# Node-ordered score columns, and a single transfer for the row maxima, in a four-layer graph network

## The chip, the cores and the metric

The kernel runs on one core of a Trainium2 chip. The metric is the device time of one execution in microseconds; lower is better. The engines are TensorE (PE; its weight loads are shown apart as PEld), VectorE (DVE), ScalarE (ACT), GpSimd (POOL) and SyncE (SP), which only issues transfers. Each runs its own instructions in order and waits for the others through semaphores. All arithmetic is in float32.

## The reference

There are B = 32 samples with N = 512 nodes and F = 64 features, and one adjacency `adj` (512 x 512, mostly zeros, with ones on the diagonal before scaling). Four residual layers follow each other: a plain graph convolution, a two-step one, a graph attention layer, and layer 3, which the change touches:

```python
def gat_layer(x, graph, W, b):
    h = x @ W
    s = jnp.einsum('bnd,bmd->bnm', h, h) * graph
    s = jnp.where(s == 0.0, NEG_INF, s)
    a = jax.nn.softmax(s, axis=2)
    return jnp.einsum('bnm,bmd->bnd', a, h) + b

h = jnp.maximum(_layernorm(x, axis=-1), 0.0)
heads = jax.vmap(lambda W, b: gat_layer(h, adj, W, b))(Wh, bh)   # 8 heads of width 128
cat = jnp.moveaxis(heads, 0, 2).reshape(B, N, H * D)
o = jax.nn.leaky_relu(cat, negative_slope=0.01)
out = gat_layer(o, adj, W_out, b_out)                           # one more, width 64
x = x + jax.nn.leaky_relu(out, negative_slope=0.01)
```

The scores of a head are symmetric before the softmax: `h h^T` with `h = x W` is `x M x^T` with `M = W W^T`, which the kernel keeps as `m2`. So a row's maximum is also the maximum of the column of the same node.

## The kernel before

Layers 0 to 2 take the first 460 us and are in a stage of their own (`slot`, `drain`). In them the change touches only `masks`, which writes `flow_neg`, a mask of -1e16 where `adj` is zero.

Nodes are laid over the 128 partitions so that node `4 p + c` sits on partition `p` in block `c` (C = 4 blocks). A row of 512 columns in **block order** holds the four nodes of a block's partitions one after the other: column `c * 128 + p`. In the **nodes' own order** it would be column `4 p + c`. Before the change every row of layer 3 is in block order.

Layer 3 is cut into 144 units, objects of a class `Pair`: 128 `Heads` (a sample and two heads at a time) and 16 `Out` (the output layer of two samples). They stand in a list `flow`, eight `Out` among the `Heads` (units 15 to 78, nine apart) and the other eight at the end. `planned` gives the order of work: the function `period(t)` is called for every t and issues, for units at different ages, what the five engines do, in an order written out by hand that is kept on every engine. `unit(k)` is the unit that is k periods old; negative ages are units that are still to come. For one unit:

- ages -4 to -1: `features`, `make_hx` (L521) make the sample's features `hx` in block order; `make_g` (L528) multiplies them by `m2`, and ScalarE copies the product from PSUM to `g` (L549). For an `Out`, `make_gs` (L621) scales the kept product `gT` by `urow` on GpSimd into `gs`.
- ages -1 and 0: `scores(r)` (L368) for the four row blocks r: TensorE multiplies a 128-column block of `terms()[0]` as weights with all 512 columns of `terms()[1]`, for two heads (k) at once. `maxima(r)` (L378) on VectorE adds the mask, turns the sign and keeps the row maximum in a column of `top`. The scores' PSUM pool `ps_s` has two buffers, which the scores share with the odd exponentials (`e_ps`).
- age 0: `spread_out` (L390): VectorE turns `top` (128 partitions x 8 used columns) in blocks of 32 x 32, and SP sends four transfers of 8 rows x 128 bytes to `top_row` in DRAM. `totals_out(0, sync)` of the unit of age 2 follows on SP (`parts`, L448), and then `spread_in` (L399), which waits for `top_row` and reads it back to all partitions as `topb`, 512 KB.
- age 1: four times `shift` (L407) on GpSimd, which subtracts `topb` from the scores column by column (the scores are used as columns, with the maximum of the column's node); `exps` on ScalarE (L416); `join` on VectorE (L419), which adds an odd block to the even block before it and frees the PSUM that the odd exponentials took. `make_v` of an `Out` (L610) transposes `gT` into the values `gV`, `gD`.
- age 2: `totals` (L432) and `values` (L421) on TensorE, `parts` to all partitions, the reciprocals, `rec_row` to DRAM (L461).
- age 3: `recb` back (L468), and `normalize` on VectorE (L474), which makes `o_att`.
- age 4: a `Heads` makes `y` and `cat` (L551 to L576), of which `product` (L596) accumulates the output layer's input, kept by `keep_product` (L606) in `gT`. An `Out` adds its bias (`bias`, L640), transposes back (`back`, L643), and at ages 5 and 6 adds to `x` on GpSimd and stores.

Three pools matter: `ps_m` (two PSUM buffers, tag "m") is shared by `g_ps`, `hx_ps`, `tot_ps`, `y_ps`, `gV_ps` and `back_ps`; `pairs_b` (L1266) holds `cat` and `y`, one buffer of 128 x 1024 in each period; `wk` holds `gs`, `topb`, `recb`, `o_att`.

Of the kernel before, what the change touches and what calls it, by code (L numbers as in the profile page):

```python
# [8 lines left out]
F32 = mybir.dt.float32  # L9
AF = mybir.ActivationFunctionType  # L10
OP = mybir.AluOpType
# [3 lines left out]
P = 128  # L15
LN_EPS = 1e-5
GAT_NEG = -9000000000000000.0
FLOW_NEG = -1e16
# [4 lines left out]
def fast_form(  # L23
# [25 lines left out]
    nc = tc.nc  # L49
    B, N, F = x.shape  # L50
    C = N // P
    H, _, D = w_heads.shape
# [3 lines left out]
    Q = P // 32  # L56

    const = ctx.enter_context(tc.tile_pool(name="const", bufs=1))
    xpool = ctx.enter_context(tc.tile_pool(name="xpool", bufs=1))
    tiny = ctx.enter_context(tc.tile_pool(name="tiny", bufs=4))  # L60
# [14 lines left out]
    adj_p = setup.tile([P, C, C, P], F32, name="adj_p")  # L75
# [37 lines left out]
    b_out2 = const.tile([P, 1], F32, name="b_out2")  # L113
# [27 lines left out]
    adj_f = adj_p.rearrange("p c k q -> p c (k q)")  # L141
    flow_neg = const.tile([P, C, N], F32, name="flow_neg")
# [15 lines left out]
    E_MAX = 5.0  # L158

    def masks():  # L160
        nc.vector.tensor_scalar(flow_neg, adj_f, 0.0, FLOW_NEG, op0=OP.is_equal, op1=OP.mult)

    root_d = const.tile([P, C], F32, name="root_d")
    urow = const.tile([P, N], F32, name="urow")
# [29 lines left out]
    def judge_rows(c):  # L194
        both, t = row_pair("edge"), row_pair("t")[:, 0]
        ok, edge = both[:, 1], both[:, 0]
        nc.vector.tensor_scalar(edge, adj_f[:, c], 0.0, None, op0=OP.not_equal)
        nc.vector.scalar_tensor_tensor(
            t, urow, root_d[:, c : c + 1], edge, op0=OP.mult, op1=OP.mult
        )  # L200
        nc.vector.tensor_tensor(t, t, adj_f[:, c], OP.subtract)
        nc.vector.scalar_tensor_tensor(t, t, -1.0, t, op0=OP.mult, op1=OP.max)
        nc.vector.scalar_tensor_tensor(
            ok, adj_f[:, c], 4e-7, t, op0=OP.mult, op1=OP.is_ge
        )
        nc.vector.scalar_tensor_tensor(
            edge, adj_t[:, c], 0.0, edge, op0=OP.not_equal, op1=OP.is_equal
        )
        nc.vector.tensor_reduce(
            sound[:, 2 + C + c : 3 + C + c], both.rearrange("p k n -> p (k n)"), AX.X, OP.min  # L210
        )

    def halves(k):
        return slice(k * F, (k + 1) * F)

    def row_pair(name):

        return pairs_of[0].tile([P, 2, N], F32, name=name, tag="row")


    acc_of, pairs_of = [], []

    def acc(name, shape):
        return acc_of[0].tile(shape, F32, name=name, tag=acc_of[1])
# [82 lines left out]
    LATE = 7  # L307
    ROOM = 6

    tops = [const.tile([P, 32], F32, name=f"top{i}") for i in range(2)]  # L310
    for t in tops:
        nc.gpsimd.memset(t, 0.0)
    ones = const.tile([P, 32], F32, name="ones32")
    nc.gpsimd.memset(ones, 1.0)

    class Pair:
# [15 lines left out]
        def make_g(self):  # L332
            pass

        def make_gs(self):
            pass

        def judge_product(self):
            pass
# [7 lines left out]
        def bias(self):  # L347
            pass
# [19 lines left out]
        def scores(self, r):  # L368
            g, x = self.terms()
            ps = ps_s.tile([P, 2, N], F32, name="s_ps", tag="s")  # L370
            self.s_ps[r] = ps
            for k in range(2):
                nc.tensor.matmul(  # L373
                    ps[:, k], lhsT=g[halves(k), r * P : (r + 1) * P], rhs=x[halves(k), :],
                    start=True, stop=True,
                )

# [10 lines left out]
                )  # L388

        def spread_out(self):  # L390
            t = tiny.tile([P, 32], F32, name="top_t")
            nc.vector.transpose(t, self.top)
            self.top_row = dram.tile([2 * C, P], F32, name="top_row")
            for q in range(Q):
                nc.sync.dma_start(
                    self.top_row[:, q * 32 : (q + 1) * 32], t[q * 32 : q * 32 + 2 * C, :]
                )

        def spread_in(self):  # L399
            self.topb = wk.tile([P, 2, N], F32, name="topb")  # L400
            nc.sync.dma_start(
                self.topb.rearrange("p k n -> p (k n)"),
                self.top_row.rearrange("(o r) p -> o (r p)", o=1).to_broadcast([P, 2 * N]),
            )

        def shift(self, r, engine):
# [69 lines left out]
    class Heads(Pair):  # L476
# [51 lines left out]
        def make_g(self):  # L528
            if self.b % 2:
                return  # L530
            pss = [acc("g_ps", [P, N]) for k in range(2)]
            for k in range(2):
                u = self.pair[k]
                u.x = Heads.hx[u.b]
                u.hnv = Heads.hn[u.b]
                u.hdv = Heads.hd[u.b]
                nc.tensor.matmul(  # L537
                    pss[k],
                    lhsT=m2[halves(k), 2 * u.i : 2 * u.i + 2, :].rearrange(
                        "p h f -> p (h f)"  # L540
                    ),
                    rhs=u.x[halves(k), :],
                    start=True,
                    stop=True,
                )
            for k in range(2):
                u = self.pair[k]
                u.g = early.tile([P, N], F32, name="g", bufs=3)
                nc.scalar.copy(u.g, pss[k])  # L549

        def y_pe(self):  # L551
            self.y = []
# [25 lines left out]
        def terms(self):  # L578
            return self.g, self.x
# [7 lines left out]
    class Out(Pair):  # L587
# [17 lines left out]

        def keep_product(self):  # L606
            self.gT = wk.tile([P, N], F32, name="gT", bufs=LATE + 1)
            nc.scalar.copy(self.gT, self.gps)

        def make_v(self):  # L610
            ps = ps_m.tile([P, C, P], F32, name="gV_ps", tag="m")
# [9 lines left out]
        def make_gs(self):  # L621
            self.gs = wk.tile([P, N], F32, name="gs")
            nc.gpsimd.tensor_tensor(self.gs, self.gT, urow, OP.mult)

        def judge_product(self):
            nc.vector.tensor_reduce(
# [2 lines left out]
            )  # L629

        def terms(self):
            return self.gs, self.gs

        def v(self, k, j):
            return self.gV[:, j, halves(k)]
# [2 lines left out]
            return self.gD[:, j // 2, halves(k)]  # L638

        def bias(self):  # L640
            nc.scalar.activation(self.o, self.o, AF.Identity, bias=b_out2, scale=1.0)

        def back(self):  # L643
            self.ps = ps_m.tile([P, C, 2, F], F32, name="back_ps", tag="m")
# [145 lines left out]
    for b in range(0, B, 2):  # L790
        out_unit = Out(b)
        for i in range(H // 2):
            pair = [Heads(b + k, i) for k in range(2)]
            for k in range(2):
                u = pair[k]
# [22 lines left out]
    with (  # L818
# [94 lines left out]
        def project(terms, tag):  # L913
            p = ps_o.tile([P, C, 2, F], F32, name=tag, tag="po")
            for c in range(C):
                for i, (t, w) in enumerate(terms):
                    nc.tensor.matmul(  # L917
                        p[:, c],
                        lhsT=t[:, c * P : (c + 1) * P],
                        rhs=w,  # L920
                        start=(i == 0),
                        stop=(i == len(terms) - 1),
                    )
            return p
# [316 lines left out]
        with tc.manual_schedule(  # L1241
            engines={
                mybir.EngineType.PE,
                mybir.EngineType.DVE,
                mybir.EngineType.Activation,
            }
        ):
            start()
            begun = {
                0: gat_weights,  # L1250
                1: edges,
                2: masks,
                3: flow_weights,
                4: scales,
            }
            for c in range(C):
                begun[6 + 2 * c] = lambda c=c: judge_rows(c)
            begun[7 + 2 * C] = judge
            for k in range(M + 1):
                slot(k, begun.get(k))  # L1260
            drain()
# [1 line left out]
    setup_ctx.close()  # L1263


    pairs_of[:] = [ctx.enter_context(tc.tile_pool(name="pairs_b", bufs=H - 2))]  # L1266
    pbuf = ctx.enter_context(tc.tile_pool(name="pbuf", bufs=4 * C - 2))

    wk = ctx.enter_context(tc.tile_pool(name="work_b", bufs=2))
    dram = ctx.enter_context(  # L1270
        tc.tile_pool(name="dram", bufs=4, space=bass.MemoryType.DRAM)
    )
# [537 lines left out]
def gnn_stack_kernel(tc: tile.TileContext, *args: bass.AP):  # L1810
    nc = tc.nc
    with tc.tile_pool(name="flag", bufs=1) as pool:
        again = pool.tile([1, 1], mybir.dt.int32, name="again")
        fast_form(tc, *args, again)
        with tc.If(nc.values_load(again[0:1, 0:1])):
            general_form(tc, *args)
# [35 lines left out]
```

## Time and profile before

| | us |
|---|---|
| median of 3 runs | 2057.39 (2053.95 to 2059.52) |
| profiled execution | 2057.15 |
| its span | 2055.4 |
| layer 3's shifts on GpSimd (L407), busy | 1338.4, in 572 instructions of 2.37 |
| layer 3's maxima on VectorE (L385), busy | 726.8, in 1152 of 0.69 |
| layer 3's scores on TensorE (L373), busy | 518.8 in 2048 records |
| transfers `top_row` | 576 of 1 KB |
| transfers `topb` | 144 of 512 KB |

"Busy" is the time in which at least one instruction of the group runs. An instruction's place in the time is read from the timeline, what it waited for from the waits; a wait for several semaphores is put down to the one that came last. Matmul ends are modelled, so the idle time of TensorE is a lower bound. A float32 matmul stands in the records as two.

### The profile page before, as it was taken

How to read it: one execution, taken by the hardware profiler on the slowest of the kernel's cores; microseconds unless marked ns; L12 is line 12 of the kernel's file. 1: busy time of each engine (PE TensorE's matmuls, PEld its weight loads, DVE VectorE, ACT ScalarE, POOL GpSimd, SP SyncE). 2: the span in 40 equal slices, each digit the busy share in tenths (PEclk: the TensorE clock that was granted, in tenths of full speed). 3: DMA queues.
4: the chain of work that ended last, by engine and by line, in shares of the span. 5: the costliest groups of instructions: out<-in, count | busy, mean ns of one | idle time of the engine just before them, and what ended most of it. 6: DMA issues, size and time to landing. Idle time of an engine off the chain costs nothing.

```text
span 2055.4 us, 32929 instructions
## 1 busy us (share of the span) xinstructions
PE 1977.7 (96%) x11038; PEld 805.5 (39%) x11038; DVE 1777.2 (86%) x4261; ACT 1221.0 (59%) x1944; POOL 1422.7 (69%) x693
## 2 busy tenths in 40 slices
PE   6999999997999999999999999999999999999995
PEld 4577766662333333333333333333333333333231
DVE  5799997768999899899989998989898898889994
ACT  3443443335666666667666667666676666665554
POOL 2000000006898989899988989898888888889996
PEclk9999999989999999999999999999999999999999
DMA  5000000002222222222222222222222222222223
GB/s 142 1 1 2 1 1 1 1 1 69 74 69 79 79 78 75 79 80 78 74 84 76 82 69 84 76 73 79 76 77 69 79 74 69 79 74 79 69 84 80
DMA packets 135780, 129.33 MB, mean 63 GB/s; under 512 B 92793, under 2 KB 98081, under 8 KB 135473
## 3 DMA queue, kind: packets, MB, share of 16 engines
q1 hardware_dynamic: 116368, 126.35, 19.5%
q10 hardware_dynamic: 18720, 0.59, 0.5%
q8 instruction: 88, 1.44, 0.3%
q0 software_dynamic: 512, 0.20, 0.1%
q14 instruction: 92, 0.75, 0.1%
HBM read 119.48 MB, written 5.37 MB: 61 GB/s over the span
## 4 chain that ended last, share of the span: by engine, by line
PE 68%; POOL 9%; DVE 9%; DMA 6%; issue 3%; ACT 3%; SPq 1%; POOLq 0%; ACTq 0%; DVEq 0%
PE s_ps L373 17%; PE av L425 16%; POOL p_att L407 9%; PE nt_ps L897 8%; PE acc L990 6%; PE tot_ps L437 4%; DVE p_att L385 4%; PE gT_ps L600 4%; PE y_ps L555 4%; PE g_ps L537 3%; DMA topb<-top_row 2%; DVE p_att L419 2%; ACT e_ps L416 1%; PE po L917 1%; DMA recb<-rec_row 1%
## 5 line engine op out<-in xcount | busy, mean ns | idle before, releaser
L407 POOL TENSOR_TENSOR p_att<-p_att,topb 128x1024 f32<-128x1024 f32 x572 | 1338.4, 2374 | 201.6 <-DMA topb<-top_row 144.2
L385 DVE CUSTOM_DVE_ANT_0 p_att<-s_ps,flow_neg 128x512 f32<-128x512 f32 x1152 | 726.8, 686 | 67.2 <-PE s_ps L373 66.2
L373 PE MATMUL s_ps<-hx,g 64*128 64x512 f32 x2048 | 518.8, 615 | 27.3 <-DVE p_att L419 25.0
L416 ACT ACTIVATE p_att<-p_att 128x1024 f32<-128x1024 f32 x288 | 304.3, 1057 | 219.7 <-POOL p_att L407 209.3
L419 DVE TENSOR_TENSOR p_att<-e_ps,p_att 128x1024 f32<-128x1024 f32 x288 | 342.4, 1200 | 66.7 <-ACT e_ps L416 65.3
L416 ACT ACTIVATE e_ps<-p_att 128x1024 f32<-128x1024 f32 x288 | 295.4, 1028 | 141.1 <-POOL p_att L407 123.3
L373 PEld LDWEIGHTS s_ps<-hx,g 64*128 64x128 f32 x2048 | 175.4, 186 | 342.2 <-DVE top L385 168.8
L425 PE MATMUL av<-p_att,hd 128*64 128x512 f32 x1024 | 269.6, 605 | 0.3 <-DVE o_att L474 0.2
L425 PE MATMUL av<-p_att,hn 128*64 128x512 f32 x1024 | 263.1, 592 | 0.0
L1066 POOL TENSOR_TENSOR x<-x,bias_b 128x512 f32<-128x512 f32 x16 | 20.3, 1276 | 282.5 <-DVE hn L839 282.5
L573 DVE SCALAR_TENSOR_TENSOR cat<-y_ps,bh,cat 128x512 f32<-128x512 f32 x256 | 179.9, 744 | 0.0
L565 ACT ACTIVATE cat<-y_ps,bh 128x512 f32<-128x512 f32 x256 | 161.7, 682 | 30.1 <-PE y_ps L555 28.4
L437 PE MATMUL tot_ps<-p_att,ones 128*32 128x512 f32 x1152 | 155.5, 604 | 4.4 <-DVE p_att L419 4.4
L555 PE MATMUL y_ps<-o_att,wh_sb 64*128 64x512 f32 x512 | 132.3, 590 | 0.0
L600 PE MATMUL gT_ps<-cat,wo_sb 128*64 128x512 f32 x512 | 131.6, 592 | 0.0
L425 PEld LDWEIGHTS av<-p_att,hn 128*64 128x64 f32 x1024 | 73.5, 137 | 146.2 <-issue 146.2
L425 PEld LDWEIGHTS av<-p_att,hd 128*64 128x64 f32 x1024 | 62.1, 136 | 165.8 <-issue 133.3
L990 PE MATMUL acc<-v,s 64*128 64x65 f32 x2048 | 123.9, 279 | 0.7 <-DVE s L976 0.4
L990 PEld LDWEIGHTS acc<-v,s 64*128 64x128 f32 x2048 | 120.9, 194 | 5.9 <-DVE o L1006 1.2
L897 PE MATMUL nt_ps<-adj_t,hn 128*128 128x512 f32 x256 | 117.0, 600 | 0.8 <-DVE hn L861 0.8
L474 DVE TENSOR_TENSOR o_att<-av,recb 128x512 f32<-128x512 f32 x144 | 94.8, 659 | 16.8 <-DMA recb<-rec_row 16.3
L549 ACT COPY g<-g_ps 128x512 f32<-128x512 f32 x128 | 69.4, 588 | 66.9 <-PE g_ps L537 66.9
(182 smaller groups left out, 1984.9 us busy)
## 6 DMA issues: line engine op xcount, KB each, us to landing
topb<-top_row SPq DMA_DIRECT2D x144, 512.0 KB
recb<-rec_row SPq DMA_DIRECT2D x288, 128.0 KB
top_row<-top_t SPq DMA_DIRECT2D x576, 1.0 KB
out_dram<-y SPq DMA_DIRECT2D x32, 128.0 KB
x<-in_x_dram SPq DMA_DIRECT2D x3, 1024.0 KB
parts<-tot ACTq DMA_DIRECT2D x144, 4.0 KB
parts<-tot SPq DMA_DIRECT2D x144, 4.0 KB
rec_row<-rec_flow SPq DMA_DIRECT2D x144, 4.0 KB
```

The costliest lines, as they stand in the source:

```text
L373: nc.tensor.matmul(ps[:, k], lhsT=g[halves(k), r * P : (r + 1) * P], rhs=x[halves(k), :], start=True, stop=True,)
L385: nc.vector.tensor_tensor_reduce(out=self.p[r][:, k], in0=ps[:, k], in1=flow_neg[:, r], scale=-1.0, scalar=BIG, op0=OP.add, op1=OP.min, ac ...
L407: engine.tensor_tensor(self.p[r], self.p[r], self.topb, OP.subtract)
L416: nc.scalar.activation(to, self.p[r], AF.Exp, scale=-1.0)
L419: nc.vector.tensor_tensor(self.p[r], self.joined, self.p[r - 1], OP.add)
L425: nc.tensor.matmul(self.av[halves(k), :], lhsT=self.v(k, j) if j % 2 else self.less_next(k, j), rhs=self.p[j][:, k], start=(j == 0), stop= ...
L437: nc.tensor.matmul(ps[q : q + 32, :], lhsT=ones, rhs=self.p[2 * e + 1][:, k], start=True, stop=True,)
L555: nc.tensor.matmul(ps, lhsT=wh_sb[halves(k), 2 * self.i + k, :], rhs=self.o[halves(k), :], start=True, stop=True,)
L573: nc.vector.scalar_tensor_tensor(self.cat[:, k], self.y[k], bh[:, h : h + 1], self.cat[:, k], op0=OP.add, op1=OP.max,)
L600: nc.tensor.matmul(self.gps[halves(k), :], lhsT=wo_sb[:, h, :], rhs=Heads.cat.pop((self.b + k, h)), start=(h == 0), stop=(h == H - 1),)
L897: nc.tensor.matmul(p, lhsT=lhs(k), rhs=adj_t[:, k, :], start=(k == 0), stop=(k == C - 1))
L990: nc.tensor.matmul(self.acc[k][:, r], lhsT=self.s[b // 2][halves(k), b % 2, r * P : (r + 1) * P], rhs=self.v[halves(k), b], start=(b == 0) ...
```

## The change

In layer 3 the columns of the scores, and all that is made from them, stand in the nodes' own order; the rows stay in block order. With that, the maxima of partition p, blocks 0 to 3, are four neighbouring words of `top_row`, and one transfer takes `top` from its partitions to DRAM in pieces of 16 bytes. For that

- `g` is written in the nodes' order by ScalarE (out of PSUM in block order), and the scores take `hx` as weights and `g` as the moving operand, where it was the other way round;
- `flow_neg` is written in the nodes' order, one block at a time;
- the transpose of `top` on VectorE and three of the four transfers go; `top` shrinks from 32 to 8 columns, and isn't cleared at the start;
- for an `Out`, the kept product is turned back to block order as it is copied (`gT`), `gs` is copied once more by ScalarE into `gn` in the nodes' order, and the bias writes a new tile in block order;
- `pairs_b` has five buffers for six.

```diff
     def masks():
-        nc.vector.tensor_scalar(flow_neg, adj_f, 0.0, FLOW_NEG, op0=OP.is_equal, op1=OP.mult)
+        for c in range(C):
+            nc.vector.tensor_scalar(
+                by_blocks(flow_neg[:, c]), adj_p[:, c], 0.0, FLOW_NEG,
+                op0=OP.is_equal, op1=OP.mult,
+            )
...
+    def by_blocks(row):
+        return row.rearrange("p (i c) -> p c i", c=C)
+
+    def in_blocks(row):
+        return row.rearrange("p (c i) -> p c i", c=C)
...
-    tops = [const.tile([P, 32], F32, name=f"top{i}") for i in range(2)]
-    for t in tops:
-        nc.gpsimd.memset(t, 0.0)
+    tops = [const.tile([P, 2 * C], F32, name=f"top{i}") for i in range(2)]
...
                 nc.tensor.matmul(
-                    ps[:, k], lhsT=g[halves(k), r * P : (r + 1) * P], rhs=x[halves(k), :],
+                    ps[:, k], lhsT=x[halves(k), r * P : (r + 1) * P], rhs=g[halves(k), :],
                     start=True, stop=True,
                 )
...
         def spread_out(self):
-            t = tiny.tile([P, 32], F32, name="top_t")
-            nc.vector.transpose(t, self.top)
-            self.top_row = dram.tile([2 * C, P], F32, name="top_row")
-            for q in range(Q):
-                nc.sync.dma_start(
-                    self.top_row[:, q * 32 : (q + 1) * 32], t[q * 32 : q * 32 + 2 * C, :]
-                )
+            self.top_row = dram.tile([2, N], F32, name="top_row")
+            nc.sync.dma_start(
+                self.top_row.rearrange("k (p c) -> p k c", c=C),
+                self.top.rearrange("p (k c) -> p k c", k=2),
+            )
...
-                nc.scalar.copy(u.g, pss[k])
+                nc.scalar.copy(by_blocks(u.g), in_blocks(pss[k]))
...
         def keep_product(self):
             self.gT = wk.tile([P, N], F32, name="gT", bufs=LATE + 1)
-            nc.scalar.copy(self.gT, self.gps)
+            nc.scalar.copy(
+                self.gT.rearrange("p (c i) -> p i c", c=C),
+                self.gps.rearrange("p (i c) -> p i c", c=C),
+            )
...
             nc.gpsimd.tensor_tensor(self.gs, self.gT, urow, OP.mult)
+            self.gn = wk.tile([P, N], F32, name="gn")
+            nc.scalar.copy(by_blocks(self.gn), in_blocks(self.gs))
...
         def terms(self):
-            return self.gs, self.gs
+            return self.gn, self.gs
...
         def bias(self):
-            nc.scalar.activation(self.o, self.o, AF.Identity, bias=b_out2, scale=1.0)
+            o = wk.tile([P, N], F32, name="o_att")
+            nc.scalar.activation(
+                o.rearrange("p (c i) -> p i c", c=C),
+                self.o.rearrange("p (i c) -> p i c", c=C),
+                AF.Identity, bias=b_out2, scale=1.0,
+            )
+            self.o = o
...
-    pairs_of[:] = [ctx.enter_context(tc.tile_pool(name="pairs_b", bufs=H - 2))]
+    pairs_of[:] = [ctx.enter_context(tc.tile_pool(name="pairs_b", bufs=H - 3))]
```

More of the change, by code (lines that the diff above doesn't have):

```diff
@@ L402, in spread_in @@
                 self.topb.rearrange("p k n -> p (k n)"),
-                self.top_row.rearrange("(o r) p -> o (r p)", o=1).to_broadcast([P, 2 * N]),
+                self.top_row.rearrange("(o k) n -> o (k n)", o=1).to_broadcast([P, 2 * N]),
             )
```

## The prediction

> **What bounds the kernel now.** I read the page's busy table first, then the windows view of the stage that the change touches, then the waits of single engines in it, and last the timeline of two units of work. "Period" is the time of one of the 144 units of layer 3.
>
> ```profile
> PE 1977.7 (96%) x11038; PEld 805.5 (39%) x11038; DVE 1777.2 (86%) x4261; ACT 1221.0 (59%) x1944; POOL 1422.7 (69%) x693
> 540.00:1940.00 1400.00, 1384.77 (x6540) 450.97 (x6536) 1261.01 (x3137) 933.41 (x1436) 1241.13 (x571) 1.00 0.25 76
> PE s_ps L373 <- DVE p_att L419: 14.4, 19, 1.2
> POOL p_att L407 <- DMA topb<-top_row: 132.5, 96, 3.8
> ```
>
> In the middle of layer 3 (540 to 1940 us, the second line: PE, PEld, DVE, ACT, POOL) TensorE is idle for only 1400 - 1384.8 = 15.2 us. Nearly all of that is one wait: the score matmuls waiting for the join L419 to free their PSUM (14.4 us, 19 times). GpSimd waits much more, 132.5 us for the maxima (`topb`), but it isn't the bound. The timeline confirms it (start, duration, engine):
>
> ```profile
> 1208.98 0.21 DVE L392 STREAM_TRANSPOSE top_t<-top 128x32 f32<-128x32 f32 x1
> 1209.22 1.35 SPq L395 DMA_DIRECT2D top_row<-top_t  x4
> 1210.62 0.57 SPq L448 DMA_DIRECT2D parts<-tot  x1
> 1211.53 0.34 SPq L401 DMA_DIRECT2D topb<-top_row  x1
> 1213.23 0.14 PEld L425 LDWEIGHTS av<-p_att,hn 128*64 128x64 f32 x2 [0.28 <-issue]
> 1213.66 0.14 PEld L425 LDWEIGHTS av<-p_att,hn 128*64 128x64 f32 x2 [0.29 <-issue]
> 1214.09 0.14 PEld L600 LDWEIGHTS gT_ps<-cat,wo_sb 128*64 128x64 f32 x2 [0.29 <-issue]
> 1214.52 0.14 PEld L600 LDWEIGHTS gT_ps<-cat,wo_sb 128*64 128x64 f32 x2 [0.29 <-issue]
> 1215.45 9.36 POOL L407 TENSOR_TENSOR p_att<-p_att,topb 128x1024 f32<-128x1024 f32 x4 [1.22 <-DMA topb<-top_row]
> 1216.64 1.07 ACT L549 COPY g<-g_ps 128x512 f32<-128x512 f32 x2 [1.35 <-PE g_ps L537]
> 1218.25 0.16 PEld L437 LDWEIGHTS tot_ps<-p_att,ones 128*32 128x32 f32 x8 [0.76 <-ACT g L549]
> 1225.64 0.34 SPq L461 DMA_DIRECT2D rec_row<-rec_flow  x1
> 1227.07 1.11 SPq L468 DMA_DIRECT2D recb<-rec_row  x2
> ```
>
> TensorE's weight loads follow each other every 0.43 us without a gap, so a period of about 10.8 us is TensorE's own work. GpSimd's four shifts take 9.36 us and start when `topb` lands. They matter at one place: the shift of row block 3 feeds the exponential, the join and then the next scores' PSUM. Where GpSimd falls behind (a unit of the output layer gives it `gs`, 1.28 us, and two sums of 0.74 us; a new pair of samples `hd`, 0.47 us), TensorE stalls. That is the 14.4 us.
>
> [...] ScalarE's reordering copy L236 reads every fourth word and takes 1130 ns, its contiguous SBUF-to-SBUF L641 710 ns for 512 elements. No run shows ScalarE writing so.
>
> **The change part by part.**
>
> 1. *The way of the maxima.* Today: last accumulate done at 1208.94, transpose 0.21 and two hand-overs (to 1209.22), four issues 1.35, `parts` 0.57, and `topb` issued at 1211.53. Over the three transfers from 1198 to 1223 the step from first issue to `topb` is 2.49, 2.31 and 2.57 us, mean 2.46; with 0.28 ahead of it, 2.74 us. Of the new transfer the nearest row is `rec_row`: 128 pieces of 32 bytes from 128 partitions, and the transfer that needs it starts 1227.07 - 1225.64 = 1.43 us after its issue. With 256 pieces I bound it by 1.43 (pieces cost nothing) and 2.86 (everything doubles) and take 1.6, because only a part of the 1.43 can be pieces. The floor on SP's queue is lower: one issue 0.34 (estimate from `rec_row`), `parts` 0.57 with 0.05 ahead and about 0.35 behind, 1.3 us. So `topb` leaves 0.05 + 1.6 = 1.65 us after the last accumulate, **1.1 us earlier**. At the upper bound it would leave 0.2 us later. `parts` too leaves about 1 us earlier, which helps the chain to `recb` (10.2 us of VectorE waiting in the same window).
> 2. *What that is worth.* Not 1.1 us a period: TensorE's work covers it. In the middle it gives GpSimd 1.1 us of lead against stalls of at most 1.2 us, so I take 13 of the 14.4 us. Outside, chains are exposed. At the start two maxima stand in series in the chain that ended last (`topb` of the first two units): 2.2 us. In the tail the last `topb` on that chain leaves 4.1 us after its accumulate (1981.49 to 1985.61): 2.5 us. GpSimd's shifts set the 40 us behind it, unchanged. Sum: 17.7 us.
> 3. *VectorE loses 144 transposes* of 0.21 us, 30 us of work. VectorE waits 59.2 us for scores in the middle, so beyond part 1 this is nothing.
> 4. *`g` is written in 16-byte strides,* 128 copies of 587 ns. Below: unchanged. Above: 1130 ns, the strided read. I take 1130. The first of two copies starts at 1216.64 and today ends at 1217.23; the totals' weights, which need its PSUM, load at 1218.25. The slack of 1.0 us covers 0.54 more. The two `g` of a pair come once in two periods, ScalarE is idle for a third of the middle. Cost: nothing; past 1.6 us a copy it would be felt.
> 5. *Output units, 16 times.* An added ScalarE copy `gn` waits for GpSimd's `gs`, which runs behind shift 3: `gs` needs 1.28 us and the exponential ahead of `gn` 1.03, so ScalarE waits 0.3 us and copies 0.7 to 1.13. Where `back_pool` stands ahead (last units) the wait is 1.8. Queued behind are the copies `gV` and `hx`, and VectorE's `gD` behind `gV`. If none were hidden, 8 x 1.4 + 8 x 2.9 = 34 us; but the next thing TensorE needs from ScalarE is 2 us or more away, and the last periods are GpSimd's. I take 0.5. The bias and the kept product may grow from 0.71 and 0.59 to 1.13; only the last bias is on the end, at most 0.4; taken 0.2.
> 6. *Masks:* one VectorE pass of 1220 ns becomes four; VectorE's own strided copies L236 take 624 ns for a quarter, so up to 2.5 us. 0 to 1.3 us once, at 45 us; I take 0.5.
> 7. *At nothing:* the swapped operands of the scores (64x128 weights and 64x512 moving, as before); the dropped memsets (setup). `pairs_b` with five buffers for six: one is taken in a period, `cat` is last read a period or two later and `y` is stored two periods later, under 30 us against 5 x 10.8. Were that cover gone, ScalarE's `cat` would wait.
>
> Sum: -17.7 + 0.5 + 0.2 + 0.5 = **-16.5 us**. The profiled execution took 2057.15 us (span 2055.4), within 0.24 of the median 2057.39. So 2057.4 - 16.5, rounded, **2041 us**.
>
> **The rivals.**
> - *The stalls are GpSimd's load, not the late maxima.* Then the middle keeps its 14.4 us and only start and tail gain: -4.7 + 1.2 = -3.5, **2054 us**. For it: three quarters of the stalls (10.9 of 14.4 us) lie before 1440 us, in the stretch where GpSimd also has `gs` and the sums. Against: GpSimd waits 132.5 us for `topb` in the same window, so it has room that it can't use. 0.12.
> - *Strided `g` holds up TensorE.* The mechanism: ScalarE's first copy of two keeps the PSUM that the totals need. It decides from 1.6 us a copy. If a scattered write costs four times the 587 ns, 2.3 us, each of 64 pairs stalls TensorE 0.7 us: +45, against -16.5, **2086 us**; at 2.0 us still +26, 2067. For it: [...] ScalarE has this slack in every second period. Against: the strided read costs 1130 ns, not 2300. Slow 16-byte pieces would end on this side too. 0.10.
> - *The maxima's transfer is no faster* (near 2.7 us): the same without the gain, about 2058 us; counted with the first rival.
>
> **How the numbers follow.** Mine 0.78, the first rival with the third 0.12, the second 0.10. A measurement of this kernel tells about 0.3% (6 us) from no change. Mine ends below that: faster 0.78; same 0.12; slower 0.10. The range runs from 2030 (all 15.2 us of idle gone, 4.7 at the ends, and some 7 us of stalls that the modelled ends of matmuls hide) to 2055, which takes in the first rival's time and leaves out little more than the slower case.
>
> **What would show it.** Right: `topb` 1.5 to 1.8 us after the issue of `top_row`; the idle of the score matmuls behind L419 in the middle down to a few us; GpSimd's wait for `topb` no longer than before, since TensorE sets the pace; `g` copies at or below 1.2 us with evenly spaced weight loads. Wrong: L419 stalls unchanged with an earlier `topb` (first rival), or weight loads of the totals that come late behind `g` (second).

## The result, and the profile after

The changed kernel takes **2050.64 us** (median; 2047.62 to 2053.44), the kernel before beside it 2057.39 (2052.40 to 2061.03): ratio **0.9970, 95% interval 0.9960 to 0.9979**. It is faster, by 6.8 us where 16.5 were forecast. Two parts of the working were wrong, and both can be seen: how early the maxima arrive and what that is worth (steps 1 and 2), and the scattered copies of `g`, which were put at nothing (step 4).

For the changed kernel: the page's busy table, the group of the copies of `g`, and the windows view of a middle stretch (columns PE, PEld, DVE, ACT, POOL).

```profile
PE 1981.8 (97%) x11038; PEld 811.8 (40%) x11038; DVE 1753.8 (86%) x4120; ACT 1296.3 (63%) x1960; POOL 1424.2 (70%) x691
L557 ACT COPY g<-g_ps 128x512 f32<-128x512 f32 x128 | 132.1, 1140 | 79.6 <-PE g_ps L545 79.6
540.00:1930.00 1390.00, 1383.15 (x6524) 455.48 (x6520) 1235.17 (x2995) 991.53 (x1443) 1236.98 (x569) 1.00 0.28 77
```

VectorE has lost its transposes. ScalarE has gained 75 us, most of it in `g` (1140 ns a copy, as taken in the prediction). TensorE is the bound as before. The waits in that stretch:

```profile
POOL p_att L415 <- DMA topb<-top_row: 115.7, 82, 3.0
DVE cat L581 <- ACT cat L573: 14.1, 21, 1.2
PE s_ps L383 <- DVE p_att L427: 6.4, 13, 1.2
SPq L409 <- DMA top_row<-top: 116.8, 114, 2.4
SPq L456 <- ACT tot L451: 24.6, 45, 0.9
```

The score matmuls wait 6.4 us behind the join, where they waited 14.4. Two waits are new: VectorE waits for ScalarE at `cat` (14.1 us), and `parts` on SP's queue waits for ScalarE's copy `tot` (24.6 us, 45 times); before, the first doesn't occur and the second stood at 0.2 us. `topb` (L409) waits for its row 116.8 us in all. Before, in the same stretch, it waited 35.3 us for its row, and `parts` 22.7 us for an exponential:

```profile
SPq L401 <- DMA top_row<-top_t: 35.3, 104, 1.8
SPq L448 <- ACT p_att L416: 22.7, 57, 0.6
```

SP now issues one transfer in place of four and is done earlier (0.38 us for 1.35), so part of that is no loss; but 114 waits in about 130 units come to 1 us each. SP's timeline shows two kinds of unit:

```profile
1203.87 0.38 SPq L402 DMA_DIRECT2D top_row<-top  x1
...
1206.43 0.32 SPq L409 DMA_DIRECT2D topb<-top_row  x1
...
1214.86 0.37 SPq L402 DMA_DIRECT2D top_row<-top  x1
...
1216.48 0.33 SPq L409 DMA_DIRECT2D topb<-top_row  x1
```

The second unit takes 1216.48 - 1214.86 = 1.62 us from the row's issue to that of `topb`, as forecast; the first takes 2.56. Over units 8 to 125 it is 1.56 at least, 2.18 in the median and 2.19 in the mean. It is above 1.9 us in 70 of these 118 units. In all 48 others and in 52 of the 70 the pieces of 16 bytes have been sent 1.1 us after the issue; what comes late in 51 of these 52 is a part of the 16 completions that the trace has for each transfer: the last comes 1.98 to 3.15 us after the issue, in the 48 within 1.82. In the other 18 late units the pieces themselves are sent late.

Where TensorE's time went is read best from the starts of its matmuls, since their ends are modelled. The sums of the intervals between neighbouring matmul records from the totals of unit 20 to those of unit 125 (105 units), in us:

| kernel | all | score to score | `y` to `y` | `g` to `g` |
|---|---|---|---|---|
| before | 1141.9 | 309.2 | 43.3 | 27.7 |
| after | 1137.8 | 300.4 | 47.9 | 27.7 |
| e1_plain_g | 1130.6 | 299.1 | 42.7 | 27.7 |
| e3_32B_pieces | 1134.9 | 297.7 | 48.0 | 27.7 |
| e6_g_by_TensorE | 1167.1 | 296.2 | 43.2 | 50.8 |
| e7_32B_right_order | 1132.5 | 295.8 | 47.7 | 27.7 |
| e11_order_in_hx | 1142.9 | 308.4 | 42.7 | 30.7 |
| e12_psum_strided | 1122.0 | 290.7 | 42.7 | 27.7 |

The pairs of neighbours that aren't shown differ by less than half a microsecond between before and after. The kernel before, profiled a second time (e5), has 1143.7, 309.6, 44.1 and 27.7 us in these columns, which shows how far equal kernels differ. So the change took 8.8 us out of the scores and put 4.7 us into `y`. Where those come from is seen in one unit, on ScalarE and on TensorE:

```profile
887.50 2.09 ACT L557 COPY g<-g_ps 128x512 f32<-128x512 f32 x2 [1.05 <-PE g_ps L545]
889.34 1.28 ACT L519 ACTIVATE hs<-hn,root_d 128x128 f32<-128x128 f32 x4
890.50 1.06 ACT L424 ACTIVATE p_att<-p_att 128x1024 f32<-128x1024 f32 x1
891.45 0.59 ACT L451 COPY tot<-tot_ps 128x512 f32<-128x512 f32 x1
891.94 1.27 PE L563 MATMUL y_ps<-o_att,wh_sb 64*128 64x512 f32 x4
```

ScalarE does the two copies of `g`, four small scalings (`hs`) and an exponential, and only then `tot`, which ends at 892.04. The second product of `y` needs the PSUM buffer that `tot` empties (`ps_m` has two, and tot, y, y follow each other). Its first record starts at 892.08, and the group takes 1.27 us where in a unit without that wait it takes 1.02. That happens in 20 of the 128 units, each time with that record 0.05 us behind the end of `tot`, and costs 5.2 us in all; before it was 3 units and 1.0 us, in e1_plain_g and e12_psum_strided it is none.

### The profile page after: what moved, and what is told of

Same layout as the page of the kernel before. It is cut to its first block, busy times and chain, and to the rows that moved or that the text cites. A ratio compares the mean times of both kernels' runs of the same rounds, so it can differ in the third digit from the quotient of the medians.

```text
span 2048.8 us, 32330 instructions
## 1 busy us (share of the span) xinstructions
PE 1981.8 (97%) x11038; PEld 811.8 (40%) x11038; DVE 1753.8 (86%) x4120; ACT 1296.3 (63%) x1960; POOL 1424.2 (70%) x691
## 3 DMA queue, kind: packets, MB, share of 16 engines
q1 hardware_dynamic: 146320, 126.34, 21.9%
## 4 chain that ended last, share of the span: by engine, by line
PE 58%; POOL 7%; DMA 4%; DVE 3%; issue 2%; ACT 2%; ACTq 0%; SPq 0%; POOLq 0%; DVEq 0%
PE s_ps L383 20%; PE av L433 19%; POOL p_att L415 7%; PE tot_ps L445 5%; PE y_ps L563 5%; PE gT_ps L608 4%; PE g_ps L545 3%; DMA topb<-top_row 2%; DVE p_att L427 1%; DMA top_row<-top 1%; DVE p_att L395 1%; ACT e_ps L424 1%; PE hx_ps L310 1%; DMA recb<-rec_row 0%; ACT p_att L424 0%
## 5 line engine op out<-in xcount | busy, mean ns | idle before, releaser
L383 PE MATMUL s_ps<-g,hx 64*128 64x512 f32 x2048 | 516.9, 614 | 19.5 <-DVE p_att L427 17.5
L383 PEld LDWEIGHTS s_ps<-g,hx 64*128 64x128 f32 x2048 | 174.9, 186 | 333.1 <-DVE top L395 173.0
L581 DVE SCALAR_TENSOR_TENSOR cat<-y_ps,bh,cat 128x512 f32<-128x512 f32 x256 | 180.1, 745 | 15.8 <-ACT cat L573 14.1
L557 ACT COPY g<-g_ps 128x512 f32<-128x512 f32 x128 | 132.1, 1140 | 79.6 <-PE g_ps L545 79.6
L563 PE MATMUL y_ps<-o_att,wh_sb 64*128 64x512 f32 x512 | 136.7, 594 | 0.0
L482 DVE TENSOR_TENSOR o_att<-av,recb 128x512 f32<-128x512 f32 x144 | 99.0, 687 | 16.7 <-DMA recb<-rec_row 15.4
```

The source lines that it names most:

```text
L383: nc.tensor.matmul(ps[:, k], lhsT=x[halves(k), r * P : (r + 1) * P], rhs=g[halves(k), :], start=True, stop=True,)
L563: nc.tensor.matmul(ps, lhsT=wh_sb[halves(k), 2 * self.i + k, :], rhs=self.o[halves(k), :], start=True, stop=True,)
L581: nc.vector.scalar_tensor_tensor(self.cat[:, k], self.y[k], bh[:, h : h + 1], self.cat[:, k], op0=OP.add, op1=OP.max,)
```

## The experiments

Each ratio is against the kernel before on the same chip. e1 to e4 share one exponential scale, -1e-20, where the change has -1 (their diffs here leave that line out). e4, whose only other edit is the mask that is made once, is therefore their control, 2049.05 us.

**e5_before_again**, the kernel before unchanged.

> The kernel before, unchanged, profiled once more. In its first profile the first matmul stands 13.05 us after the start of the span, in the five profiles of changed kernels 9.05 to 9.4. If that was chance of the first loads: 9 to 10 us here and a span about 2051. If something in the changed kernels speeds the loads: near 13 again. Either way, if the accounts of the stage hold, units 20 to 125 take 1142 us within 1.5 and the idle of the score matmuls behind the join is near 14 us.

2055.59 us. Its first matmul starts 8.7 us after the span's start, as in every later profile (after: 9.1), and not 13.05 as in the first profile of before. Those 4 us of the first load are chance, and so part of the difference between the two first profiles is none of the change's. Units 20 to 125 took 1143.7 us and the scores waited 15.4 us behind the join, near what was expected; the span, 2053.8, was 3 us longer than expected.

### The way of the maxima

**e2_old_row**: no `topb` but the first waits for its own unit's row; it reads that of the unit before.

```diff
-                self.top_row.rearrange("(o k) n -> o (k n)", o=1).to_broadcast([P, 2 * N]),
+                row.rearrange("(o k) n -> o (k n)", o=1).to_broadcast([P, 2 * N]),
```

> The changed kernel with topb read from the row of the unit before, which has long landed (maxima of the wrong unit; the exponentials' scale is -1e-20 to keep them finite). topb then leaves as soon as SyncE's queue lets it, about 1.2 us after top_row's issue instead of 2.2. T1: the idle of the score matmuls in the middle falls from 6.4 to 3 us or less and the kernel gains 3 to 6 us more on before, 9 to 13 in all. T2: the idle stays near 6 us, and the gain stays at 6 to 7 us.

2044.10 us, ratio 0.9936 (0.9921 to 0.9952). Row to `topb` 1.35 us in the mean; the score matmuls wait 3.7 us behind the join for the 6.4 of the change. That is T1: 13 us below before, and 5 below the control.

**e3_32B_pieces**: the same bytes in 128 pieces of 32.

```diff
-                self.top_row.rearrange("k (p c) -> p k c", c=C),
-                self.top.rearrange("p (k c) -> p k c", k=2),
+                self.top_row.rearrange("k (p i) -> (k p) i", i=2 * C), self.top,
```

> The changed kernel with the maxima's row written as 128 pieces of 32 bytes, a partition's eight words together (their order in the row is then wrong; exponentials' scale -1e-20). If the length or number of the pieces is what makes the completions late: topb leaves 1.5 to 1.9 us after top_row's issue on the mean, as recb after rec_row (1.73), against 2.19 now, and the kernel gains 1 to 4 us on the changed one. If it is what else runs on the queues at that time: 2.1 us or more, no gain.

2043.12 us, 0.9931 (0.9915 to 0.9946): 6 us below the control, as much as where no `topb` waits for its own row (e2). Row to `topb` 1.66 us in the mean, 1.48 in the median. So the pieces are what makes most of these completions late; whether by their number or by their size, no run separates.

**e7_32B_right_order**: the same, with `topb` laid out as the row comes (node, head, block), and GpSimd reading it in runs of four words.

```diff
-            self.top_row = dram.tile([2, N], F32, name="top_row")
+            self.top_row = dram.tile([P, 2 * C], F32, name="top_row")
...
-            engine.tensor_tensor(self.p[r], self.p[r], self.topb, OP.subtract)
+            p = self.p[r].rearrange("p k (i c) -> p k i c", c=C)
+            engine.tensor_tensor(
+                p, p, self.topb.rearrange("p (i k c) -> p k i c", k=2, c=C), OP.subtract
+            )
```

> The changed kernel with 128 pieces of 32 bytes and topb kept as they lie (node, head, block), GpSimd's subtraction reading it in runs of four words; same result. If GpSimd's reading costs nothing: 2.37 us a shift, topb leaves about 1.66 us after top_row's issue, the kernel is within 2 us of the one with 32-byte pieces, 2043. If runs of four words cost GpSimd time: over 2.6 us a shift, four of them over 10.4 us a unit, and the kernel is slower than before.

**2038.74 us, 0.9917 (0.9903 to 0.9930)**, better than both kernels. The waits of this kernel in the same stretch, and two lines of SP's timeline:

```profile
DVE cat L581 <- ACT cat L573: 15.3, 25, 1.2
PE s_ps L383 <- DVE p_att L427: 1.3, 3, 1.0
SPq L406 <- DMA top_row<-top: 44.4, 88, 2.0
```

```profile
1208.46 0.32 SPq L402 DMA_DIRECT2D top_row<-top  x1
...
1209.92 0.33 SPq L406 DMA_DIRECT2D topb<-top_row  x1
```

`topb` waits 44.4 us for its row where it waited 116.8, and 1.46 us pass between the two issues (mean 1.61). The stalls behind the join are all but gone; the wait at `cat` is as it was, since `g` is still scattered. The subtraction keeps its 2375 ns. The page counts 127888 packets on queue q1 for the change's 146320, which is 144 x 128 fewer: 128 pieces a row for 256. e3, with the same transfer, has a median 4.4 us higher; the two intervals of the ratios overlap, so that difference is not clear of the noise.

### The copies of `g`

**e1_plain_g**: the change, with `g` copied straight.

```diff
-                nc.scalar.copy(by_blocks(u.g), in_blocks(pss[k]))
+                nc.scalar.copy(u.g, pss[k])
```

> The changed kernel with g copied straight, not in 16-byte strides (its columns then stand in block order, so the attention is another; the exponentials' scale is set to -1e-20 to keep them finite). Theory T1 (the completion of the 16-byte pieces eats the lead of the maxima): ScalarE's copies fall from 1.14 to 0.59 us, and the time stays within 2 us of the changed kernel, about 6 us below before; the score matmuls' idle behind the join between 540 and 1930 us stays near 6 us. Theory T2 (the strided copies hold ScalarE, it holds VectorE's cat, and that keeps the stalls): VectorE's wait for cat (14 us) goes, the idle falls to 2 us or less, the kernel is 10 us or more below before.

2042.79 us, 0.9937 (0.9919 to 0.9954): 6 to 8 us below the control and the change. The waits:

```profile
PE s_ps L383 <- DVE p_att L427: 5.3, 13, 0.9
DVE cat L581 <- ACT cat L573: 2.5, 8, 0.3
SPq L456 <- ACT tot L451: 1.9, 5, 0.6
```

Both new waits go (14.1 to 2.5, 24.6 to 1.9), and the `y` to `y` intervals fall to 42.7 us. T1, which expected no gain, is out; T2 is right that the copies hold ScalarE and cost time, and wrong that they keep the stalls behind the join. These stay at 5.3: that is the other cause.

**e6_g_by_TensorE**: `hx` is read in the nodes' order by the matmul that makes `g`.

```diff
-                    rhs=u.x[halves(k), :],
+                    rhs=in_nodes(u.x[halves(k), :]),
...
-                nc.scalar.copy(by_blocks(u.g), in_blocks(pss[k]))
+                nc.scalar.copy(u.g, pss[k])
```

> The changed kernel with g put in the nodes' order by TensorE (hx is read as the moving operand with a stride of 512 bytes in the product that makes g) and copied straight by ScalarE; same result. T2: the second of two y matmuls no longer waits (that row of intervals goes back from 47.9 to 43 us over units 20 to 125), the kernel is within 2 us of the one with the plain copy, 2043. If TensorE pays for the strided operand: the g matmuls' intervals (27.7 us for these units) grow, and up to all of the gain is lost, 2050.

2085.63 us, **1.0143 (1.0128 to 1.0159), slower**. The `y` to `y` intervals are back at 43.2 us, but the moving operand, read at a distance of 512 bytes, costs TensorE far more than it saves: besides `g` to `g` (27.7 to 50.8) the intervals from `g` to the scores grow from 20.5 to 38.0 us in the 105 units. Both expected times were too low. The matmuls of `g` in this kernel, and then in e7:

```profile
L548 PE MATMUL g_ps<-hx,m 64*128 64x512 f32 x232 | 120.0, 1080 | 0.0
```

```profile
L545 PE MATMUL g_ps<-hx,m 64*128 64x512 f32 x236 | 71.0, 641 | 0.0
```

**e8_both**, e6 and e7 together:

> Both corrections together: g ordered by TensorE, 32-byte pieces. T1 and T2 each took about 7 us of the expected gain; if they add, 2036 to 2038. If the stalls that they leave are the same ones, 2041 to 2043, no better than either alone.

2080.18 us, 1.0121 (1.0105 to 1.0136). Scores 293.8 and `y` 42.7 us in the 105 units, `g` to `g` still 50.8: both cures work, and TensorE's new work outweighs them. The expectation, written before the result of e6, leaves that work out.

**e11_order_in_hx**: e7 with the order made in `hx`, and `g` copied straight; `block` gives the scores' weights.

```diff
-                nc.scalar.copy(by_blocks(u.g), in_blocks(pss[k]))
+                nc.scalar.copy(u.g, pss[k])
...
+        def block(self, x, r):
+            return x.rearrange("p (i c) -> p c i", c=C)[:, r]
```

> e7_32B_right_order, with the nodes' own order made where hx is copied out (16 scattered ScalarE copies in place of 128 of g): g is copied straight, and the scores' stationary operand, the block r of hx, is read at a distance of 16 bytes by the weight load. The same result. Theory A (ScalarE's scattered g copies are what the new order costs; weight loads lie beside the matmuls): g copies at 590 ns, the g and s rows as in e7, the second y's row back from 47.7 to about 43 us in 105 units, VectorE's wait at cat for ScalarE back to 2 to 3 us; 2038.7 less 5 to 7, near 2033, the fastest of all; weight loads longer than 186 ns but hidden. Theory B (a scattered read costs a weight load what it cost the moving operand, 641 to 1080 ns for 512 columns, and the load cannot hide all of it): the intervals of the score matmuls grow by 0.05 us or more each, 1856 of them, some 90 us: above 2100 us.

2055.49 us, 0.9992 (0.9984 to 1.0001): neither number. The wait at `cat` went (2.7 us), yet all that e7 had gained went too. The scores' weight loads, here and then in e7:

```profile
L386 PEld LDWEIGHTS s_ps<-g,hx 64*128 64x128 f32 x1912 | 279.7, 310 | 217.5 <-DVE top L398 135.9 <-DVE p_att L430 42.2 <-issue 6.3
```

```profile
L383 PEld LDWEIGHTS s_ps<-g,hx 64*128 64x128 f32 x1912 | 162.7, 185 | 289.2 <-DVE top L395 162.4 <-DVE p_att L427 72.9 <-issue 48.9
```

310 ns in place of 185, 117.0 us in all (279.7 - 162.7). Most of that is hidden, as theory A had it, and 12.6 us of it (308.4 - 295.8 in 105 units) isn't; no score matmul waits for the join in 540 to 1930 of this run (0.0 us), so the join isn't what holds them.

**e12_psum_strided**: e7, with the same copy walked the other way.

```diff
-                nc.scalar.copy(by_blocks(u.g), in_blocks(pss[k]))
+                nc.scalar.copy(
+                    u.g.rearrange("p (i c) -> p i c", c=C),
+                    pss[k].rearrange("p (c i) -> p i c", c=C),
+                )
```

> e7_32B_right_order with the g copies walked the other way: ScalarE writes g word after word and reads the PSUM at a distance of 512 bytes, in place of reading PSUM in order and writing at a distance of 16 bytes. The same result. Theory A (it is the scattered write to SBUF that costs, PSUM may be read in any order): the copy falls from 1140 to about 590 ns, the wait of VectorE at cat for ScalarE from 15 to 2 or 3 us, the second y's row from 47.7 to 43 us in 105 units; 2038.7 less 5 to 7, near 2033, the fastest of all. Theory B (any scattered operand costs ScalarE the same): 1090 to 1140 ns, as the copies of gT take, which write at 512 bytes; the time as e7, 2037 to 2041.

**2026.39 us (2025.20 to 2028.09), 0.9842 (0.9829 to 0.9855)**: the best of all, 24 us below the change. Its groups and windows, and its waits:

```profile
L557 ACT COPY g<-g_ps 128x512 f32<-128x512 f32 x128 | 69.5, 588 | 110.8 <-PE g_ps L545 110.8
540.00:1930.00 1390.00, 1389.63 (x6612) 455.07 (x6608) 1243.30 (x3037) 956.49 (x1454) 1255.07 (x578) 1.00 0.26 78
```

```profile
DVE cat L584 <- ACT cat L576: 2.7, 8, 0.4
PE s_ps L383 <- DVE p_att L427: 0.3, 1, 0.3
SPq L456 <- ACT tot L451: 0.8, 2, 0.5
```

Word after word written, the copy takes 588 ns, what the straight copy takes in the kernel before (588), with the PSUM read at a distance of 512 bytes. Theory A holds in its mechanism; the gain over e7 is 12.4 us for its 5 to 7. TensorE is busy for 1389.63 of 1390 us. Against the change, quick maxima alone gain 11.9 us (e7) and the straight copy alone 7.9 (e1; 6.3 against its control); e12, with both, gains 24.3, where the two add to 19.8. In the 105 units the gains are 5.3, 7.2 and 15.8 us. The likely reason, which no run tests alone, is that both causes feed the same stalls, since a late exponential on ScalarE makes the join late as a late shift on GpSimd does: VectorE's wait for the exponential at the join is 54.6 us before, 38.1 after, 19.5 in e7 and 14.6 here.

### Smaller questions

**e10_idle_transposes**: the change with VectorE's 144 transposes put back as idle work, in `spread_out` behind the row's transfer.

```diff
+            nc.vector.transpose(idle_t, idle_s)
```

> The changed kernel with the 144 transposes of VectorE put back as idle work: behind the issue point of the maxima's row, on a tile of zeros, read by nobody. Theory A (step 3: the 30 us that the transposes took on VectorE are worth nothing in themselves; only the way of the row counted): 2050.6, ratio to the changed kernel 1.000 within 0.1%, the score stalls behind the join near 6.4 us. Theory B (VectorE's free time behind the maxima shortens the joins, for which the score matmuls wait): each unit's joins come about 0.2 us later; with two thirds of the 116 middle units feeling it the time is 10 us or more longer, near 2060, and the wait of the score matmuls for the join is back at 14 us or above.

2047.40 us, 0.9956 (0.9939 to 0.9973), certainly not slower than the change. The group and the wait in 540 to 1930:

```profile
L409 DVE STREAM_TRANSPOSE idle_t<-idle_s 128x32 f32<-128x32 f32 x129 | 26.7, 207 | 0.0
```

```profile
PE s_ps L386 <- DVE p_att L431: 7.3, 17, 1.2
```

The transposes stand there with their 207 ns and stop nobody: score to score 300.4 us, as in the change.

**e9_before_32B**: the kernel before, with only the maxima's way changed, so that nothing is scattered by ScalarE, and GpSimd reads `topb` word by word.

```diff
+            p = self.p[r].rearrange("p k (c i) -> p k c i", c=C)
+            engine.tensor_tensor(
+                p, p, self.topb.rearrange("p (i k c) -> p k c i", k=2, c=C), OP.subtract
+            )
```

> The kernel before with its own order of the columns (g copied straight, the mask in one pass) and only the way of the maxima changed: no transpose on VectorE, the row goes out in one transfer of 128 pieces of 32 bytes, and the subtraction reads topb word by word at a distance of 32 bytes. Theory A (two independent effects: the faster way takes the score stalls away, and ScalarE's scattered g copies are a cost of their own that only the new order brings): the gain of e7_32B_right_order (0.9917) and that of e1_plain_g over the change (0.9970 to 0.9937, 0.33%) add up: 0.988, about 2033 us, the fastest of all; score stalls behind the join at 1 to 3 us in 540 to 1930, the wait of VectorE at cat for ScalarE back to 2 to 3 us, g copies at 590 ns. Theory B (an operand that touches 4 bytes in each 32 slows GpSimd as the scattered write slowed ScalarE, 587 to 1140 ns): the subtraction goes from 2375 ns to some 4600 ns, 518 times, GpSimd becomes the bound and the time goes far beyond 2300 us. Theory C (the two effects overlap): no better than e7, 2036 to 2042.

2179.17 us, **1.0591 (1.0570 to 1.0611), slower**. Theory B in kind, at 0.28 of its size (620 ns more for 2225):

```profile
L401 POOL TENSOR_TENSOR p_att<-p_att,topb 128x1024 f32<-128x1024 f32 x480 | 1368.0, 2995 | 1.4 <-DMA topb<-top_row 0.8 <-issue 0.4
```

Each shift takes 2995 ns for 2375, and GpSimd, which now waits 1.4 us in 1390, is the bound. So the new column order is not a detour: with it the layout that one transfer leaves is read in runs of four words (e7), at 2375 ns a shift.

**e4_plain_mask**: the change, with the mask in one pass of VectorE.

```diff
-        for c in range(C):
-            nc.vector.tensor_scalar(by_blocks(flow_neg[:, c]), adj_p[:, c], 0.0, FLOW_NEG,
-                                    op0=OP.is_equal, op1=OP.mult)
+        nc.vector.tensor_scalar(flow_neg, adj_f, 0.0, FLOW_NEG, op0=OP.is_equal, op1=OP.mult)
```

> The changed kernel with the mask made in one pass as before (its columns in block order, so masked entries are others; exponentials' scale -1e-20). The first score matmul of layer 3 stands 445.41 us after the first matmul in the changed kernel, 444.26 before. If the four strided passes are the cause: back to within 0.3 of 444.3, the time 1 us less. If not: stays at 445.4.

2049.05 us, 0.9964 (0.9951 to 0.9977), inside the change's interval. From the first matmul to the first score matmul 445.3 us, in the change 445.4; e3 and e7, which don't differ from the change up to there, have 446.0 and 444.4. The mask's cost can't be seen.

## Why the prediction was wrong, step by step

- **The bound and the mechanism: right.** TensorE sets the pace, and its stalls behind the join were partly the late maxima: 14.4 to 6.4 us with the change, to 1.3 with a row that is really quick (e7). The first rival (stalls are GpSimd's load) is out: GpSimd's shifts are as many and as long in e7 and e12, and the stalls are 1.3 and 0.3 us.
- **Step 1, the way of the maxima: mis-sized.** 1.6 us from the row to `topb` holds for the undisturbed units (1.62 above) and not for the mean, 2.19. From the last accumulate to `topb` the mean went from 2.96 to 2.22 us in units 8 to 125: 0.74 earlier, not 1.1. `rec_row` was the nearest row, but it has pieces of 32 bytes, and its 1.43 us came from one unit. Over units 8 to 125 of the same trace it is 1.42 us at least and 1.94 in the mean: 1.99 in the 108 units where a `topb` was issued less than 2.5 us before it, 1.45 in the other ten. So pieces of 32 bytes can be late too, and the working had the best case for the usual one. Its 2.46 us for the step of today, from three units, is 2.69 in the mean.
- **Step 2, the worth: wrong in all three terms.** The middle's waits lost 8.0 us, not 13. At the start and in the tail nothing came: from the first score matmul to the totals of unit 20 it took 241.8 us before and after, from the totals of unit 125 to the end 214.3 and 214.7. At the start, VectorE's own maxima and the shift behind them set the chain of the first unit, and the second unit's row was a late one (2.5 us). In the tail, `topb` on the chain leaves 3.7 us after its last accumulate where 4.1 passed before, because this row was a late one, and GpSimd's shifts set most of what follows:

```profile
1974.76 3.59 DMA top_row<-top
...
1993.83 9.33 POOL p_att L415 x4
...
2037.25 1.19 ACT o_att L655
```

- **Step 3, VectorE's transposes at nothing: right** (e10).
- **Step 4, scattered `g` at no cost: the second failure.** It cost 4.7 us in the 105 units. The duration was right (1140 ns for 1130), and so was the totals' PSUM: no totals are late. The step looked at the first user of ScalarE's next buffer and stopped there. Behind the copies stood `hs`, an exponential and `tot`, and behind `tot` the second `y`. By the medians it is 6 to 8 us (e1), and 12.4 where the maxima are quick (e12 against e7). This is the second rival's mechanism one tenant of the pool later, and far below the 1.6 us a copy that the rival named; its four times 587 ns was an assumption that no trace showed, and 1140 ns is 1.9 times.
- **Step 5, output units, 0.7 us: about right, its last bias too low.** The last bias, the last line above, took 0.73 us before: 0.46 more at the end, where 0.2 was taken and 0.4 named as the most. For the rest, e12 keeps their scattered copies (1163 ns for `gn`, 1198 for the bias) and stalls 0.3 us.
- **Step 6, masks:** no cost to be seen (e4). **Step 7:** the swapped operands cost nothing (score to score, e12 has the shortest intervals in the table, with the operands swapped); no wait for the buffers of `cat` or `y` in `pairs_b` shows.

So the trace supports, for the 105 units, -8.8 (scores) + 4.7 (`y`) = -4.1 us, with nothing gained at the ends. The spans of the two first profiles differ by 6.5 us: 4.0 of the first load, which is chance, 4.1 in the 105 units, less 1.1 ahead of the first score matmul and 0.4 in the tail. Against the second profile of before (e5) the difference is 5.0 us, with 5.9 in the 105 units. The medians say 6.8; the 1 to 3 us between that and the 105 units can't be placed, since single profiles of equal kernels differ by as much.

The reason why completions of 16-byte pieces come late in more than half of the units stays open. What is shown is that twice the size and half the number nearly ends it: in e7, 9 of the 118 units stand above 1.9 us, in the change 70.

## What to carry to other kernels

When a change makes one engine's instruction longer, follow that engine's queue to the buffer after next: the user that pays may be several instructions behind (here the second `y`, behind `tot`: 4.7 us in 105 units). If ScalarE must reorder data on its way from PSUM to SBUF, scatter the side in PSUM and write SBUF word after word (588 ns here for 1140); and if an order is made in SBUF reads, look which engine has to pay (TensorE's moving operand did, 1080 ns for 641 in e6; GpSimd's runs of four words didn't, 2375 ns in e7). Two small causes can each look cheap to leave, and be worth more together than their sum (24.3 us here for 19.8). Take a wait that varies as a mean over many units, not from one.

## What was unexpected of the hardware

- How long a transfer of 4 KB kept the next one waiting went with its pieces, and not only with the time of sending them. With 256 of 16 bytes the next transfer, which needs it, was issued 2.19 us after it in the mean, with 128 of 32 bytes 1.61 (the change and e7); and in 52 of the change's 70 late units the pieces had been sent 1.1 us after the issue, as in the 48 others.
- TensorE paid for strides in SBUF: a moving operand of 512 columns at 512 bytes took 1080 ns for 641 (e6 and e7; `g` to `g` in the 105 units 50.8 us for 27.7), a weight load of 128 columns at 16 bytes 310 ns for 185 (e11 and e7).
- GpSimd read runs of four words at no cost (2375 ns in e7, 2374 before), and single words at 32 bytes for 26% more (2995 ns, e9).
- ScalarE read PSUM at 512 bytes at no cost (588 ns in e12, 588 before), and took longer when it wrote SBUF at 16 bytes (`g`, 1140 ns for 588) or at 512 (`gT`, 1086 ns for 586; the change and before).
